# Sums over neighbours as seven half-size products in growing banks, in a two-layer graph kernel

## The chip, the cores and the metric

The kernel runs on one core of a Trainium2 chip. The metric is the device time of one execution in microseconds (us). Engines are named as in the profile: PE (TensorE), PEld (its weight loads), DVE (VectorE), ACT (ScalarE), POOL (GpSimd), SP (the queue that issues most transfers).

## What is computed

64 graphs of 256 nodes with 512 features, all in float32. With `ln` the layer norm, layer 0 is an attention masked by the adjacency matrix, layer 1 a graph convolution:

```
h = relu(ln(x));  q, k, v = h Wq' + bq, h Wk' + bk, h Wv' + bv
w = adj * exp(q k');  x = x + (w / rowsum(w)) v
h = relu(ln(x));  A = adj + I;  d = rowsum(A) ** -0.5
x = x + (d A d) (h W + b)          # d A d: rows and columns scaled by d
```

## The kernel before

**Tiles.** A round handles a pair of graphs (32 pairs, `p`). A pair's x is one tile of 128 partitions x 4 x 512: index t = 2 * node block + graph. The adjacency of the pair, `a`, and its transpose, `aT` (node block of the neighbour, graph, 256 nodes), are tiles too.

**Seven products.** Most matrix products are done on 2 x 2 blocks with seven block products in place of eight (the Winograd form). Sums of blocks (`s1..s4`, `t1..t4`) are made ahead of it, and the block results are put together from three PSUM banks. A bank "grows": a first product is written into it, somebody reads it, and a later product is added to the same bank. `seven_products` (L341) fixes the order: bank 0: A11, then A12; bank 1: S2, S3, A22; bank 2: S1, S4. After each product a callback reads the bank on ACT or DVE, and what the callback is told to start (`then_first`, `then_u2`, ...) is work for another pair, put into the queue behind that reading with `tc.issue_after`. [...]these callbacks set the order of all side work.

**Stages of pair p, in the order of TensorE.**

- `attend(p)` (L490): scores of both graphs in seven products of 128 columns (`pm_s`, L504), exponentials on ACT, masks with `aT` on DVE (L528), then eight tiles of weighted values (`pm_o`, L562). Then POOL adds the identity to the diagonal blocks of `aT` (L814), issues the transfer that adds the value bias to the next x, and makes the scale and offset of the second norm (`scale_offset`, L243: statistics on DVE, a chain of small POOL steps `irs_b` to `nb_b`, ending in L259).
- `project(p+1)` (L761): the key side (`pm_g`, seven products of 256 columns), and then the values (`pm_v`, seven products, `values` L429). Beside it: ACT's second norm of pair p (`h_b`, L266); statistics and degrees of pair p+2 on DVE and POOL (`irs_a` to `nb_a`); key sums on POOL (L334 to L338); ACT's first norm of pair p+2 (`h_a`); its transposes of 32 x 32 blocks on DVE (`hq`, L291), which ACT moves into place (`hT`, L310); four steps of key terms on DVE (`hc`, L280); and last, on DVE, the graph bias times the weighted degree, added to x of pair p (`add_graph_bias`, L610).
- `second_layer(p)`, `convolve` (L614): four sums over neighbours, each in a bank of its own (`pm_l`, L625), 16 matmuls of 256 columns; their sums (`yS`) on ACT and DVE; then seven products with the graph weight (`pm_w`, L358). Behind the last sum, t4, stands `weighted_degrees` of pair p+1 on DVE (`ad`, L593). In the products: ACT's scaled copies and the second half of the moves for pair p+2, POOL's additions to x (L667), DVE's scaled additions (L660), DVE's transposes of the next adjacency (`aT`, L475), then POOL's feature sums for pair p+2 (L320 to L324).

The last pairs differ: convolve(30) and convolve(31) follow each other, with the second norm of pair 31 in the former and its graph bias in the latter. In the first round the sums of the graph weight (L154 to L157), the weighted degrees of pair 0 and the transposed adjacency of pair 1 stand behind the value products on DVE. A tile's name after `tag=` is its slot: tiles of one tag share it, and a pool's `bufs` says how many slots there are. All PSUM tiles take turns in 8 banks.

## Time and profile before

| | |
|---|---|
| median of 3 runs | 1845.81 us (1845.35 to 1845.84) |
| the profiled execution | time 1845.12 us, span 1843.3 us |
| granted TensorE clock | 0.999 |
| one round, from attention to attention | 56.4 us (903.94 to 960.31) |
| of it `attend`: scores | 903.94 to 910.21 |
| weighted values | 910.21 to 917.14 |
| key side and values | 917.14 to 941.32 |
| sums over neighbours | 941.32 to 948.22 |
| graph weight's products | 948.22 to 960.31 |

The profile is of one execution. A timeline row has the start in us from the span's start, the length in us, the engine, the line and operation, what is written and read, the shape and how many instructions are merged in it; in brackets the idle time ahead of it and what ended that. A float32 matmul shows as two records, each with a weight load. Matmul ends are modelled and overlap the next start, so times of TensorE are read from start to start.

### The profile page before, as it was taken

The page shows a single profiled execution, that of the slowest core. Times are in us where ns is not written, and L with a number is a line of the kernel's source. Part 1 is how long each engine was busy: PE and PEld are TensorE (multiplying, and loading weights), DVE is VectorE, ACT ScalarE, POOL GpSimd, SP SyncE. Part 2 cuts the span into 40 slices and gives each one's busy share as a digit, 9 for nine tenths or more (in the row PEclk, how much of TensorE's full clock was granted, in tenths as well). Part 3 has the DMA queues.
Part 4 walks back from the last instruction along what each step waited for, and adds up shares of the span by engine and source line. Part 5 has one row for each costly group of instructions (what it writes and reads, how often), then busy time and mean ns, then how long its engine had stood idle before and what let it go on. Part 6 is the DMA issues. An engine that isn't in the chain of part 4 may idle for free.

```text
span 1843.3 us, 25928 instructions
## 1 busy us (share of the span) xinstructions
PE 1831.0 (99%) x9346; PEld 1632.8 (89%) x9346; DVE 1297.7 (70%) x3102; ACT 801.7 (43%) x1476; POOL 690.0 (37%) x867
## 2 busy tenths in 40 slices
PE   9999999999999999999999999999999999999999
PEld 8888888888888888888888888888888888888887
DVE  6877676676766767766767667677667677676755
ACT  4444444345434444443454344444434543444422
POOL 2433334333344333343333443433433334434332
PEclk9999999999999999999999999999999999999999
DMA  8343234332233432343422344223443223342111
GB/s 229 52 98 83 53 67 96 92 97 64 52 86 92 97 82 50 69 98 92 96 61 57 86 92 98 80 50 72 98 92 97 58 59 86 92 98 79 36 36 46
DMA packets 224192, 148.29 MB, mean 80 GB/s; under 512 B 150208, under 2 KB 170688, under 8 KB 224064
## 3 DMA queue, kind: packets, MB, share of 16 engines
q1 hardware_dynamic: 206048, 112.03, 22.2%
q0 software_dynamic: 16960, 33.56, 11.9%
q8 instruction: 74, 1.21, 0.3%
q10 hardware_dynamic: 1056, 1.05, 0.2%
q14 instruction: 54, 0.44, 0.1%
HBM read 112.99 MB, written 33.62 MB: 80 GB/s over the span
## 4 chain that ended last, share of the span: by engine, by line
PE 97%; DVE 1%; DMA 1%; issue 0%; POOL 0%; ACTq 0%; DVEq 0%
PE pm_w L358 21%; PE pm_g L358 21%; PE pm_v L358 20%; PE pm_o L562 12%; PE pm_l L625 12%; PE pm_s L504 11%; PE pm_mT L175 1%; DMA wq_rows<-in_L_gnn_Wq_w_dram 1%; DMA dflat<-irr_d 0%; DVE hc L280 0%; DVE ad L593 0%; DVE hq L291 0%; PE pt_h L300 0%; PE pt_wv L225 0%; DVE deg L578 0%
## 5 line engine op out<-in xcount | busy, mean ns | idle before, releaser
L358 PE MATMUL pm_w<-w_set,yS 128*128 128x256 f32 x1792 | 392.0, 379 | 0.0
L358 PEld LDWEIGHTS pm_w<-w_set,yS 128*128 128x128 f32 x1792 | 340.5, 190 | 46.3
L310 ACT COPY hT<-hq 32x512 f32<-32x512 f32 x496 | 305.4, 616 | 31.8 <-DVE hq L291 26.0
L358 PE MATMUL pm_v<-v_set,hT 128*128 128x256 f32 x1024 | 241.7, 379 | 0.0
L358 PE MATMUL pm_g<-hT,m_set 128*128 128x256 f32 x1024 | 236.7, 379 | 0.0
L667 POOL TENSOR_TENSOR x<-x,A_w 128x512 f32<-128x512 f32 x32 | 40.6, 1269 | 516.8 <-ACT A_w L658 516.8
L562 PE MATMUL pm_o<-v,wT 128*128 128x257 f32 (+1 forms) x1024 | 228.0, 380 | 0.0
L625 PE MATMUL pm_l<-aT,h_b 128*128 128x256 f32 x1024 | 226.2, 379 | 0.0
L358 PEld LDWEIGHTS pm_g<-hT,m_set 128*128 128x128 f32 x1024 | 194.5, 190 | 27.0 <-issue 0.5
L625 PEld LDWEIGHTS pm_l<-aT,h_b 128*128 128x128 f32 x1024 | 194.6, 190 | 26.5
L358 PEld LDWEIGHTS pm_v<-v_set,hT 128*128 128x128 f32 x1024 | 194.5, 190 | 26.4
L562 PEld LDWEIGHTS pm_o<-v,wT 128*128 128x128 f32 x1024 | 191.9, 190 | 26.8 <-DVE wT L528 0.3
L358 PE MATMUL pm_g<-hS,m_set 128*128 128x256 f32 x768 | 181.3, 379 | 0.0
L358 PE MATMUL pm_v<-v_set,hS 128*128 128x256 f32 x768 | 176.6, 379 | 0.0
L660 DVE SCALAR_TENSOR_TENSOR x<-pm_w,irr_d,x 128x256 f32<-128x256 f32 x256 | 110.9, 474 | 75.3 <-PE pm_w L358 75.3
L358 PEld LDWEIGHTS pm_g<-hS,m_set 128*128 128x128 f32 x768 | 145.4, 190 | 20.5 <-DVE U_g L398 0.3
L358 PEld LDWEIGHTS pm_v<-v_set,hS 128*128 128x128 f32 x768 | 145.8, 190 | 19.9
L390 ACT COPY A_g<-pm_g 128x512 f32<-128x512 f32 x32 | 18.7, 585 | 234.1 <-PE pm_g L358 233.4
L667 POOL TENSOR_TENSOR x<-x,U_w 128x512 f32<-128x512 f32 x64 | 81.2, 1269 | 102.0 <-DVE x L660 102.0
L266 ACT ACTIVATE h_b<-x,nb_b,rs_b 128x512 f32<-128x512 f32 x128 | 93.7, 803 | 47.6 <-POOL nb_b L259 47.6
L572 DVE SCALAR_TENSOR_TENSOR x<-pm_o,rsum,x 128x256 f32<-128x256 f32 x256 | 110.5, 473 | 2.0 <-DVE rsum L570 1.1
L436 ACT COPY A_v<-pm_v 128x512 f32<-128x512 f32 x32 | 18.7, 585 | 206.1 <-PE pm_v L358 197.1
(141 smaller groups left out, 2633.8 us busy)
## 6 DMA issues: line engine op xcount, KB each, us to landing
x<-in_x_dram SPq DMA_DIRECT2D x64, 512.0 KB, 4.9
x<-in_L_gnn_Wv_b_dram POOLq DMA_DIRECT2D x32, 1024.0 KB, 9.8
out_dram<-x SPq DMA_DIRECT2D x62, 512.0 KB, 3.0
a<-in_adj_dram SPq DMA_DIRECT2D x64, 256.0 KB, 2.9
aq<-in_adj_dram SPq DMA_DIRECT2D x124, 128.0 KB, 4.5
drow<-dflat SPq DMA_DIRECT2D x32, 256.0 KB, 4.7
wq_rows<-in_L_gnn_Wq_w_dram ACTq DMA_DIRECT2D x2, 512.0 KB, 7.5
wk_rows<-in_L_gnn_Wk_w_dram SPq DMA_DIRECT2D x2, 512.0 KB, 6.8
```

What stands on the lines that cost most here:

```text
L175: nc.tensor.matmul(pm, wk_rows[:, oc, ts(dc, P)], wq_rows[:, oc, ts(half, HD)], start=oc == 0, stop=oc == DC - 1,)
L266: nc.scalar.activation(h[:, t, :], x_tiles[p][:, t, :], AF.Relu, bias=nb[:, t : t + 1], scale=rd[:, t : t + 1],)
L310: last = nc.scalar.copy(dst[j * Q : (j + 1) * Q, i], src[i * Q : (i + 1) * Q, j])
L358: nc.tensor.matmul(banks[bank][:, r, :], left[:, ts(r, P)], right, start=start and r == 0 and dt == 0, stop=r == 1 and dt == 1, skip_group ...
L390: with tc.issue_after(nc.scalar.copy(a1, pm).ins):
L436: with tc.issue_after(nc.scalar.copy(a1, pm).ins):
L504: nc.tensor.matmul(banks[bank][:, g, :], left[:, dt, ts(g, P)], right[:, dt, ts(g, P)], start=start and g == 0 and dt == 0, stop=g == 1 an ...
L562: nc.tensor.matmul(pm[:, 0:width], wT[:, kb, qb, g, :], v[:, kb * G + g, lo : lo + width], start=kb == 0, stop=kb == NB - 1,)
L572: nc.vector.scalar_tensor_tensor(xh, pm[:, 0:HD], rsum, xh, mult, add)
L625: nc.tensor.matmul(pm[:, fi, :], h[:, jb * G + g, ts(2 * fh + fi, P)], aT[:, jb, g, :], start=jb == 0, stop=jb == NB - 1,)
L660: last = nc.vector.scalar_tensor_tensor(dst[:, r, :], pm[:, r, :], dr_, plus[:, r, :], mult, add)
L667: last = nc.gpsimd.tensor_tensor(block(i, g), block(i, g), more, add).ins
```

## The change

The sums over neighbours become seven products of half size, with new block sums on POOL (`neighbour_sums`), and are read from growing banks, in one hand-written order with the graph weight's products. In `convolve`, blocks of x are now taken by node block in place of by graph. `t3` and `t4` move from DVE to POOL. The weighted degrees of a pair move to its own value stage (`then_c22`), the graph bias to behind the key side. In the first round, the weighted degrees of pair 0 go into project(1), the transposed adjacency of pair 1 too, and the sums of the graph weight go to POOL. The scratch tiles of `hc` and `ad` take slot A0, the attention's small tiles become one tile in slot `hq`. The core of the diff:

```diff
-        scratch = p1.tile([P, D], F32, tag="scratch", name=f"hc_{p}")
+        scratch = p1.tile([P, D], F32, tag="A0", name=f"hc_{p}")
...
+        hold = p1.tile([P, 4, G, P], F32, tag="hq", name=f"hold_{p}")
-        first, u2, u3, c22 = (small(tag) for tag in ("sA", "sU2", "sU3", "sC"))
+        first, u2, u3, c22 = (hold[:, i] for i in range(4))
...
+    def neighbour_sums(p, h, aT):
+        a11, a21 = h[:, 0:G, 0:HD], h[:, 0:G, HD:D]
+        a12, a22 = h[:, G:TB, 0:HD], h[:, G:TB, HD:D]
+        gS = p1.tile([P, 3, G, HD], F32, tag="hbS", name=f"hbS_{p}")
+        s1, s2, s4 = (gS[:, i] for i in range(3))
+        b11, b12 = (aT[:, 0, :, ts(i, P)] for i in range(2))
+        b21, b22 = (aT[:, 1, :, ts(i, P)] for i in range(2))
+        aS = p1.tile([P, 3, G, P], F32, tag="aS", name=f"aS_{p}")
+        t1, t2, t4 = (aS[:, i] for i in range(3))
+        eng = nc.gpsimd
+        eng.tensor_tensor(t1, b12, b11, sub)
+        eng.tensor_tensor(t2, b22, t1, sub)
+        eng.tensor_tensor(s1, a21, a22, add)
+        eng.tensor_tensor(s2, s1, a11, sub)
+        eng.tensor_tensor(a21, a11, a21, sub)
+        eng.tensor_tensor(b12, b22, b12, sub)
+        eng.tensor_tensor(t4, b21, t2, sub)
+        eng.tensor_tensor(s4, a12, s2, sub)
+        return (a11, a12, a22, s1, s2, a21, s4), (b11, b21, b22, t1, t2, b12, t4)
...
-        pm11 = aggregate(0, 0)
-        with tc.issue_after(moved) if moved else ExitStack():
-            nc.scalar.copy(b11, pm11)
-        pm12 = aggregate(0, 1)
-        nc.vector.tensor_tensor(t1, pm12, b11, sub)
-        pm22 = aggregate(1, 1)
-        nc.scalar.copy(b22, pm22)
-        nc.vector.tensor_tensor(t2, pm22, t1, sub)
-        nc.vector.tensor_tensor(t3, b22, pm12, sub)
-        pm21 = aggregate(1, 0)
-        nc.scalar.copy(b21, pm21)
-        with tc.issue_after(nc.vector.tensor_tensor(t4, pm21, t2, sub).ins):
-            then_t4()
...
+        def gather(bank, left, right, start=False):
+            if start:
+                banks[bank] = ps_m.tile([P, 2, G, P], F32, tag="pm", name=f"pm_l_{p}_{bank}")
             for fi in range(2):
+                for g in range(G):
                     nc.tensor.matmul(
+                        banks[bank][:, fi, g, :],
+                        left[:, g, ts(fi, P)],
+                        right[:, g, :],
...
+        chain = gather(0, a11, c11, True)
+        with tc.issue_after(moved) if moved else ExitStack():
+            nc.scalar.copy(b11, chain)
+        pm = gather(1, a12, c21, True)
+        nc.vector.tensor_tensor(b11, pm, b11, add)
+        gather(0, s2, u2)
+        nc.vector.tensor_tensor(part, chain, b11, sub)
+        rest = gather(2, s1, u1, True)
+        gather(0, s3, u3)
+        nc.scalar.copy(three, chain)
+        pm0 = product(0, A11, b11, True)
+        nc.vector.tensor_tensor(b22, rest, three, add)
+        nc.scalar.copy(a, pm0)
+        gather(0, a22, u4)
+        nc.scalar.copy(b21, chain)
+        gather(2, s4, c22)
+        nc.vector.tensor_tensor(t1, rest, part, add)
+        last = nc.vector.tensor_tensor(t2, b22, t1, sub)
+        nc.gpsimd.tensor_tensor(t3, t2, b11, sub)
+        turned = nc.gpsimd.tensor_tensor(t4, b21, t2, sub)
+        with tc.issue_after(last.ins):
+            then_t2()
+        scaled(a1, a, 1)
+        last = scaled(a, a, 0)
+        with tc.issue_after(turned.ins):
             into(1, 0, None, a)
+        with tc.issue_after(last):
+            then_first()
+        product(0, A12, b21, False)
+        into(0, 0, pm0)
+        pm2 = product(2, S1, t1, True)
+        pm1 = product(1, S2, t2, True)
+        s2, s3 = (temp(tag, f"w{p}") for tag in ("U2", "U3"))
+        scaled(s2, pm1, 1, a1)
+        into(0, 1, None, s2)
+        product(1, S3, t3, False)
+        with tc.issue_after(scaled(s3, pm1, 1, a1)):
+            then_u3()
+        into(1, 1, pm2)
+        last = into(1, 1, None, s3)
+        product(1, A22, t4, False)
+        into(1, 0, pm1)
+        product(2, S4, b22, False)
+        into(0, 1, pm2)
...
     def project(p, then_g):
+        def then_u2():
+            ahead(measure, p + 1)()
+            if p == 1:
+                weigh_degrees(0)
+        keys[p], last = key_side(p, parts[p], then_g, then_u2, nothing)
+        with tc.issue_after(last):
+            add_graph_bias(p - 1)
         key_parts[p] = key_sums(p, keys[p])
+        if p == 1:
+            weight_sums(w1_set, w1_21, nc.gpsimd)
+        def then_c22():
+            if p == 1:
+                aTs[1] = transposed_adjacency(1)
+            weigh_degrees(p)
-        last = values(
+        values(
...
             then_u3=ahead(find_terms, p + 1),
+            then_c22=then_c22,
         )
-        with tc.issue_after(last.ins):
-            add_graph_bias(p - 1)
...
     def finish_second_norm(p):
-        second[p] = normed(p, f"b{p}", *norms[p])
+        second[p] = neighbour_sums(p, normed(p, f"b{p}", *norms[p]), aTs[p])
```

The scheduler that places the instructions keeps this order on DVE, ACT and POOL with small shifts: on DVE the four `hc`, the four `ad` and three value steps stand between U_v (s3) and `b11`'s addition, and on POOL the order after `nb_b` is s1, s2, the difference in a21, s4, then `irs_a` to `nb_a`, then the key sums.

## Prediction

> **What bounds the kernel now.** I read the page's busy shares and chain first, then the TensorE timeline of one middle pair, then VectorE's and GpSimd's timelines of that pair, and last the one place where TensorE really waits, the first pair.

> ```profile
> PE 1831.0 (99%) x9346; PEld 1632.8 (89%) x9346; DVE 1297.7 (70%) x3102; ACT 801.7 (43%) x1476; POOL 690.0 (37%) x867
> ...
> PE 97%; DVE 1%; DMA 1%; issue 0%; POOL 0%; ACTq 0%; DVEq 0%
> PE pm_w L358 21%; PE pm_g L358 21%; PE pm_v L358 20%; PE pm_o L562 12%; PE pm_l L625 12%; PE pm_s L504 11%; PE pm_mT L175 1%; DMA wq_rows<-in_L_gnn_Wq_w_dram 1%; DMA dflat<-irr_d 0%; DVE hc L280 0%; DVE ad L593 0%; DVE hq L291 0%; PE pt_h L300 0%; PE pt_wv L225 0%; DVE deg L578 0%
> ```

> TensorE sets the end, and it is full: only fewer streamed columns can help, and any new wait costs in full. The TensorE timeline of a middle pair (start, length, then line and tiles) prices the columns:

> ```profile
> 903.94 1.05 PE L504 MATMUL pm_s<-hT,gT 128*128 128x128 f32 x8
> 904.83 1.95 PE L504 MATMUL pm_s<-hS,gS 128*128 128x128 f32 x16
> ...
> 941.32 7.07 PE L625 MATMUL pm_l<-aT,h_b 128*128 128x256 f32 x32
> 948.22 12.25 PE L358 MATMUL pm_w<-w_set,yS 128*128 128x256 f32 x56
> ```

> From start to start, 8 records of 128 columns take 0.89 us (112 ns each; a float32 matmul is two records), 32 of 256 columns take 6.90 (216 ns each). So half-width costs a little over half.

> **The gain.** The sums over neighbours were 32 records of 216 ns = 6.90 us a pair. They become seven products of 4 matmuls of 128 columns: 56 x 112 = 6.27 us. Gain 0.63 us a pair, 32 x 0.63 = 20 us. The other products are the same in number and width. Without new waits this would give 1825 us.

> **The waits that pay for it.** Before, every neighbour sum had its own bank and TensorE asked nobody. Now bank 0 grows: it is read by ScalarE (b11), by VectorE (`part`), by ScalarE (`three`), each time before TensorE may go on. So VectorE's queue ahead of `part` comes onto TensorE's path. In it stand the four key terms hc (L280), and now also the weighted degrees (ad, L593), moved there from behind t4. VectorE and GpSimd in this stretch before:

> ```profile
> 936.34 0.69 DVE L448 TENSOR_TENSOR U_v<-pm_v,A_v 128x512 f32<-128x512 f32 x1 [0.31 <-PE pm_v L358]
> 936.95 0.68 DVE L280 SCALAR_TENSOR_TENSOR hc<-h_a,c_all 128x512 f32<-128x512 f32 x1
> ...
> 925.43 0.23 POOL L238 TENSOR_SCALAR irs_a<-mv_a 128x4 f32<-128x4 f32 x1 [4.28 <-DVE mv_a L250]
> ...
> 928.12 0.20 POOL L259 TENSOR_TENSOR nb_a<-nm_a,irr_a 128x4 f32<-128x4 f32 x1
> 930.88 1.27 POOL L334 TENSOR_TENSOR gS<-gT 128x512 f32<-128x512 f32 x1 [2.57 <-DVE gT L409]
> ...
> 934.71 1.26 POOL L338 TENSOR_TENSOR gS<-gT,gS 128x512 f32<-128x512 f32 x1
> ```

> The key sums on GpSimd (L334 to L338) end at 935.97, one microsecond before the first hc. That gap matters, as the first pair shows, where feature sums on GpSimd run beside hc and ad:

> ```profile
> 53.99 1.66 DVE L280 SCALAR_TENSOR_TENSOR hc<-h_a,c_all 128x512 f32<-128x512 f32 x1
> ...
> 56.21 1.12 DVE L280 SCALAR_TENSOR_TENSOR hc<-h_a,c_all 128x512 f32<-128x512 f32 x1
> ...
> 53.83 1.27 POOL L320 TENSOR_TENSOR hS<-hT 128x512 f32<-128x512 f32 x1 [11.42 <-ACT hT L310]
> 55.18 1.60 POOL L321 TENSOR_TENSOR hS<-hT,hS 128x512 f32<-128x512 f32 x1
> ...
> 59.21 1.16 PE L504 MATMUL pm_s<-hT,gT 128*128 128x128 f32 x8 [2.54 <-DVE sU L533]
> ```

> An hc of 0.68 us takes 1.66: it starts 0.16 after L320 and ends 0.55 after it. The next is held to the end of L321. [...]for operands from PSUM and for the block transposes, which overlap GpSimd's sums in every pair, it shows no lengthening. [...]

> Now the middle pair's timetable, in the times of before. GpSimd's queue: after nb_b come four neighbour sums, which wait for ScalarE's h_b (ends 924.12). Priced as the key sums (5.09), they end at 929.3. Only then follow irs_a to nb_a (2.89 before, from 925.43). VectorE's bias step (4 STT, 2.73 us as L610) now runs at 930.7 to 933.4, directly after the key side. It holds back irr_d and nb_a (0.7 together, the nearest being the small GpSimd steps of the first pair, lengthened by 0.2 to 0.5 each): nb_a ends near 933.0 instead of 928.3. Hence
> - the key sums run from 933.3 to about 938.35, over the first hc;
> - ScalarE's h_a (began 931.68) begins at 933.05, so the four transposes end at 936.8 instead of 936.0, and U_v (s3) starts at 936.7 instead of 936.34;
> - the first hc would start at 937.3, is held to 938.2 and ends 938.9; the second 939.6; c22 (0.69) ends at 940.25. TensorE's last value product reuses c22's bank and would start at 939.59. Wait 0.7, with restart **0.8 us**. (A restart after a short wait costs 0.07: at 1793.1, after 0.62 us idle, one matmul took 185 ns and the next 112.)
> - then hc 0.73, hc 0.61, c21 0.61, ks 0.22, ad 0.46 and 0.36, c12 0.61, ad 0.46 and 0.47, s 0.19, b11 0.61, ds 0.19, `part` 0.69: `part` ends at 946.4. TensorE, restarted at 940.4, has the product (1.73) and four gathers (3.58) and is there at 945.7. Wait 0.7, with restart **0.8 us**. Were no GpSimd step in the way, the same sum from 936.34 would end at 945.1 against 944.9: 0.3 us remain.
> - b21: the last gather of bank 0 is copied by ScalarE (0.585), which has just done a's copy and one scaling (0.58 + 0.43); it ends about 0.1 after TensorE's next gather. **0.2 us** (0 to 0.3).
> - the A22 product waits for VectorE's reading of s3 (two STT, 0.88) behind half a product: **0.1 us** (0 to 0.2).
> - In the attention, the first adjacency sum (128x256: 0.73 us, estimated between 0.46 for 128x128 and 1.27 for 128x512) enters GpSimd right after the first two diagonals, at 910.70; the mask of block (1,0) came at 910.80. If the sum is first, the mask ends 0.45 later, and pm_o's fourth matmul waits 0.35; if the mask is first, the sum holds the next masks and the statistics behind them, and all of the chain above comes later. **0.3 us** (0 to 0.45).

> Sum 2.2 us of waits against 0.63: +1.57 a pair, for the 29 pairs with this order (it is the same in all of them): +45.5 us.

> Costed at nothing: t3 and t4 moved to GpSimd (2 x 1.27, idle there, a product of 1.73 ahead of S3; without that cover 1.2 us), the fifth VectorE step, scratch tiles sharing A0 and hq (same engines), the output and load DMAs (same order on SP; x is not read sooner). h_b is not held up: the other adjacency sums end near 916.5, and irs_b comes at 919.06.

> The ends. The first pair loses work from VectorE: its attention waits 2.54 and 1.64 us, and then runs at half rate (213 ns per record) for about 2 us, 6.4 us in all. But the graph weight's sums go to GpSimd, 4 x 1.27 beside the same hc, so I take 3 of it (0 to 6.4). Pair 0's own sums follow a longer VectorE queue (two more transposes, 1.3): +2. Pair 30 has no hc ahead of it: -0.3. In pair 31 the bias (2.73) stands between t2 and the steps that free bank 1, and t3, t4 on GpSimd interleave with it: about 3.3 of wait, net +2.7 (0 to 3.5). Together +1.4.

> The sum is made against the profiled execution: span 1843.3, time 1845.1, which is 0.7 below the median of the runs, 1845.8. 1845.1 + 45.5 + 1.4 = **1892 us**.

> **Rivals.**
> - *A, as above*, 1870 to 1915: chance 0.62.
> - *B, the queues miss each other*: the key sums end before hc, and the masks go first. Left are 0.3 (`part`), 0.2, 0.1, 0.3 = 0.9, net +0.3 a pair: 29 x 0.3 + 1.4 = +10, 1855 (1847 to 1870). For it: the gap between sums and hc is one microsecond now. Against: GpSimd's order puts 5.1 us ahead of nb_a. Chance 0.20.
> - *C, faster: the gain comes through*. If VectorE reaches `part` by 944.9, no bank is late, and 20 us are gained, with the first pair's 3 to 6: 1820 to 1825, up to 1841 with a part of it. It decides at one place, the start of the third gather into bank 0: VectorE must be 0.3 us earlier than the best that I find. For it: all other growing banks (pm_g, pm_v, pm_w, pm_s) run without waits. Against: none of them has hc and ad ahead of it. Chance 0.09.
> - *D, worse*: a key sum gets in ahead of the fourth bias step; U_v (s2) is then 1.2 later, at 935.2, and the value product on bank 1 (934.41) waits 0.85 more: 29 x 0.85 = +25, 1917 (1915 to 1935). Chance 0.09.

> That the change does not do what it says is excluded by the matmuls of its program: 28 of 128 columns a pair.

> **Numbers.** The range 1850 to 1920 takes A whole, most of B and a little of D; about 2 in 10 stay out. A measurement tells about 0.2% (3.7 us) from no change. Faster 0.09 (C), within 0.2% 0.04 (B's lower end), slower 0.87.

> **What would show it.** TensorE busy near 1811 with 60 or more us of idle; rows of waits "pm_v <- v" at the last value product and "pm_l <- U_l" at the third gather of bank 0, each about 0.7 us in some 29 places; hc's mean up from 697 to about 900 ns; pm_l records 112 ns apart. Wrong: no idle before pm_l, or hc at 0.68 throughout (B or C); idle ahead of pm_v's S3 product (D).

## The result and the profile after

The changed kernel takes **1896.78 us** (median of four runs, 1895.71 to 1898.62), beside 1845.82 of the kernel before on the same chip (1845.35 to 1847.0): a ratio of 1.0276 (95% interval 1.0258 to 1.0294), slower. The profiled execution has a span of 1894.9 us against 1843.3, 51.6 more, at a granted clock of 0.997. The forecast was 1892.

The busy shares and the chain of the page of after:

```profile
PE 1852.5 (98%) x10114; PEld 1642.0 (87%) x10114; DVE 1358.7 (72%) x3130; ACT 797.9 (42%) x1476; POOL 1070.3 (56%) x1191
...
PE 73%; DVE 25%; issue 1%; POOL 1%; DMA 1%; ACT 0%; DVEq 0%; ACTq 0%; POOLq 0%
```

TensorE had 97% of the chain and now has 73%; the 25% that VectorE took over are its queue, followed back from where TensorE waits for it in every pair (a share of the chain, not the length of the waits). Now TensorE's timeline of the same middle pair (its key side begins 21.38 us later than before):

```profile
961.38 1.99 PE L358 MATMUL pm_v<-v_set,hT 128*128 128x256 f32 x8 [0.25 <-DVE v L458]
963.21 1.95 PE L654 MATMUL pm_l<-aT,h_b 128*128 128x128 f32 x16
965.03 2.02 PE L654 MATMUL pm_l<-aS,hbS 128*128 128x128 f32 x16
967.37 1.13 PE L654 MATMUL pm_l<-aT,h_b 128*128 128x128 f32 x8 [0.31 <-DVE U_l L696]
```

16 records of 128 columns take 1.82 us from start to start, so the half-size products do run at their price. Two brackets are new, and they stand where the forecast put them: ahead of the last value product and ahead of the third gather of bank 0. The brackets undercount: the modelled end of a record of 256 columns lies 0.16 us behind the start of the next, and the second record after a wait comes late too (by 0.10 and 0.07 here). From start to start the two waits are 0.53 and 0.55 us. VectorE and GpSimd in this pair:

```profile
958.37 0.67 DVE L281 SCALAR_TENSOR_TENSOR hc<-h_a,c_all 128x512 f32<-128x512 f32 x1
...
959.09 1.63 DVE L281 SCALAR_TENSOR_TENSOR hc<-h_a,c_all 128x512 f32<-128x512 f32 x1
...
960.65 0.68 DVE L458 TENSOR_TENSOR v<-pm_v,U_v 128x512 f32<-128x512 f32 x1
...
966.53 0.69 DVE L696 TENSOR_TENSOR U_l<-pm_l,yS 128x512 f32<-128x512 f32 x1
...
953.62 0.54 POOL L260 TENSOR_TENSOR nb_a<-nm_a,irr_a 128x4 f32<-128x4 f32 x1
954.12 1.78 POOL L335 TENSOR_TENSOR gS<-gT 128x512 f32<-128x512 f32 x1
...
958.46 1.71 POOL L339 TENSOR_TENSOR gS<-gT,gS 128x512 f32<-128x512 f32 x1
```

The last key sum (L339, 1.71 us where it took 1.26 before) is held by the first hc and then holds the second: it ends at 960.17, and that hc, begun at 959.09, takes until 960.72. c22 (L458) starts when hc is done, and the value product behind it; `part` (U_l) ends at 967.22, and the third gather starts 0.15 later. Over the whole run (us in total, times, longest):

```profile
PE pm_l L654 <- DVE U_l L696: 10.6, 30, 1.2
PE pm_v L358 <- DVE v L458: 7.5, 29, 0.3
```

One round by stages, each the mean over 26 middle pairs from the start of a record to the start of the next (so a wait is counted in the stage of the record before it; worked out from the trace; "v3" comes further below):

```
us per pair             pm_o   pm_g   pm_v   pm_l   pm_w   pm_s   period
before                  6.93  12.09  12.09   6.91  12.09   6.27   56.37
after                   7.32  12.09  12.61   6.99  12.34   6.37   57.72
e1 key sums later       7.32  12.09  12.10   6.65  12.34   6.37   56.87
e2 mask first           6.93  12.09  12.61   6.99  12.34   6.37   57.33
e3 split product        7.32  12.09  12.61   6.43  12.34   6.37   57.16
e4 no block sums        6.93  12.09  16.04   6.61  12.34   6.37   60.38
e5 ends                 7.32  12.09  12.61   6.97  12.34   6.37   57.71
e6 c22 first            7.32  12.09  12.09   6.42  12.35   6.37   56.63
e10 same, order kept    7.32  12.09  12.09   6.78  12.34   6.37   56.98
e7 degrees back         7.32  12.10  12.64   6.64  16.32   6.41   61.42
e8 same, other slot     7.32  12.09  12.61   6.64  14.14   6.37   59.17
e9 norm first           6.93  12.09  16.49   7.20  12.34   6.37   61.42
v3 all                  6.93  12.09  12.09   6.43  12.14   6.26   55.95
```

After minus before is +1.345 a pair, 39 us over 29 pairs. The other 12.6 lie at the ends: 2.3 up to the second pair's weighted values (the first pair's start 2.7 earlier, then 5.0 are lost), 1.8 between pairs 30 and 31, 7.6 from there to the last product, 0.9 behind it. Each of e1 to e10 below is one run; the kernel before gave 1845.1 to 1846.3 beside them.

### The profile page after: what moved, and what is told of

Same layout as the page of the kernel before. It is cut to its first block, busy times and chain, and to the rows that moved or that the text cites. A ratio compares the mean times of both kernels' runs of the same rounds, so it can differ in the third digit from the quotient of the medians.

```text
span 1894.9 us, 27986 instructions
## 1 busy us (share of the span) xinstructions
PE 1852.5 (98%) x10114; PEld 1642.0 (87%) x10114; DVE 1358.7 (72%) x3130; ACT 797.9 (42%) x1476; POOL 1070.3 (56%) x1191
## 3 DMA queue, kind: packets, MB, share of 16 engines
q10 hardware_dynamic: 1056, 1.05, 0.2%
## 4 chain that ended last, share of the span: by engine, by line
PE 73%; DVE 25%; issue 1%; POOL 1%; DMA 1%; ACT 0%; DVEq 0%; ACTq 0%; POOLq 0%
PE pm_w L358 21%; PE pm_g L358 20%; PE pm_s L511 10%; PE pm_o L566 10%; DVE hc L281 6%; PE pm_v L358 6%; PE pm_l L654 5%; DVE hq L292 4%; DVE ad L597 3%; DVE x L614 2%; DVE wT L532 1%; DVE U_l L696 1%; DVE yS L694 1%; DVE U_v L446 1%; DVE v L472 1%; DVE v L471 1%
## 5 line engine op out<-in xcount | busy, mean ns | idle before, releaser
L358 PE MATMUL pm_w<-w_set,yS 128*128 128x256 f32 x1792 | 413.2, 386 | 3.8 <-DVE U_w L674 3.8
L358 PEld LDWEIGHTS pm_w<-w_set,yS 128*128 128x128 f32 x1792 | 332.4, 191 | 57.3 <-issue 10.4
L708 POOL TENSOR_TENSOR yS<-yS 128x512 f32<-128x512 f32 x32 | 41.1, 1284 | 410.1 <-DVE yS L707 410.1
L358 PE MATMUL pm_v<-v_set,hT 128*128 128x256 f32 x1024 | 245.2, 382 | 10.3 <-DVE v L458 7.5
L358 PE MATMUL pm_g<-hT,m_set 128*128 128x256 f32 x1024 | 238.5, 381 | 4.2 <-DVE gT L415 4.2
L566 PE MATMUL pm_o<-v,wT 128*128 128x257 f32 (+1 forms) x1024 | 235.3, 382 | 3.5
L358 PEld LDWEIGHTS pm_v<-v_set,hT 128*128 128x128 f32 x1024 | 192.3, 190 | 47.5 <-DVE v L458 19.2
L358 PEld LDWEIGHTS pm_g<-hT,m_set 128*128 128x128 f32 x1024 | 195.7, 191 | 31.9 <-DVE gT L415 5.0
L358 PE MATMUL pm_g<-hS,m_set 128*128 128x256 f32 x768 | 181.2, 379 | 1.0 <-DVE U_g L404 1.0
L358 PE MATMUL pm_v<-v_set,hS 128*128 128x256 f32 x768 | 176.8, 379 | 0.0
L358 PEld LDWEIGHTS pm_g<-hS,m_set 128*128 128x128 f32 x768 | 145.7, 190 | 21.3 <-DVE U_g L404 1.4
L358 PEld LDWEIGHTS pm_v<-v_set,hS 128*128 128x128 f32 x768 | 146.0, 190 | 19.7
L684 POOL TENSOR_TENSOR x<-x,U_w 128x512 f32<-128x512 f32 x64 | 81.0, 1267 | 93.5 <-DVE U_w L674 93.5
L674 DVE SCALAR_TENSOR_TENSOR U_w<-pm_w,irr_d,A_w 128x256 f32<-128x256 f32 x128 | 56.0, 480 | 98.8 <-PE pm_w L358 98.8
L281 DVE SCALAR_TENSOR_TENSOR hc<-h_a,c_all 128x512 f32<-128x512 f32 x128 | 115.9, 905 | 2.0
L654 PE MATMUL pm_l<-aT,h_b 128*128 128x128 f32 x768 | 98.6, 278 | 10.6 <-DVE U_l L696 10.6
```

Of the source, the lines that this page charges most:

```text
L281: nc.vector.scalar_tensor_tensor(scratch, h[:, t, :], 1.0, c_all, mult, mult, accum_out=acc[:, t : t + 1])
L358: nc.tensor.matmul(banks[bank][:, r, :], left[:, ts(r, P)], right, start=start and r == 0 and dt == 0, stop=r == 1 and dt == 1, skip_group ...
L566: nc.tensor.matmul(pm[:, 0:width], wT[:, kb, qb, g, :], v[:, kb * G + g, lo : lo + width], start=kb == 0, stop=kb == NB - 1,)
L654: nc.tensor.matmul(banks[bank][:, fi, g, :], left[:, g, ts(fi, P)], right[:, g, :], start=start and fi == 0 and g == 0, stop=fi == 1 and g ...
L674: last = nc.vector.scalar_tensor_tensor(dst[:, r, :], pm[:, r, :], dr_, plus[:, r, :], mult, add)
L684: last = nc.gpsimd.tensor_tensor(block(i, nb), block(i, nb), more, add).ins
```

## The experiments

**Theory T.** The half-size products themselves are cheaper (16 records in 1.82 us). What costs is a meeting on two engines: the neighbour sums push the key sums on GpSimd later (1.9 us at their start, 2.8 at their end), over hc on VectorE, and there VectorE's steps with two SBUF inputs and GpSimd's sums hold each other up, as seen above: hc takes 1.63 us in place of 0.68, the key sum 1.71 in place of 1.26. VectorE's steps that read PSUM and its block transposes were not held in the kernel before: U_v (L440) took 0.69 us in all 32 pairs, in 31 of them beside a GpSimd sum, and the 124 transposes (L291) 0.67 to 0.71, 120 of them beside such sums. VectorE then comes late to two readings that TensorE now waits for. **Rival R:** VectorE has simply got too much work ahead of `part`, or GpSimd has too many sums, wherever they lie.

### e1: the key sums elsewhere

```diff
-        nc.vector.tensor_tensor(ds, s, d, mult)
+        last_ds[0] = nc.gpsimd.tensor_tensor(ds, s, d, mult).ins
...
-        key_parts[p] = key_sums(p, keys[p])
...
+        with tc.issue_after(last_ds[0]):
+            key_parts[p] = key_sums(p, keys[p])
```

The new place is behind `values(p)`; the other small step of the degrees, `s`, goes to GpSimd in the same way.

> The changed kernel with the four key sums on GpSimd issued later, behind the last step of the weighted degrees (some 945 to 949 in the pair's timetable, where GpSimd is idle), in place of beside bias, hc and U_v; the last two small steps of the degrees (128x4) go to GpSimd to give that place in the queue. Everything else is as changed. Theory T (the key sums exclude hc on VectorE; that is what makes TensorE wait at the last value product and at the third gather of bank 0): hc back to 0.70 us mean from 0.905, the wait ahead of the last value product (0.52 a pair) and that ahead of pm_l (0.55 a pair) both go, 1.07 x 29 = 31 us less than the changed kernel's 1897: 1866. Rival R (VectorE simply has too much to do ahead of `part`; who runs beside it does not matter): only the two small steps are saved, 1893.

Measured: 1867.22 us. hc in the groups by line (busy us, mean ns, idle before), and the first key sum in GpSimd's timeline:

```profile
L282 DVE SCALAR_TENSOR_TENSOR hc<-h_a,c_all 128x512 f32<-128x512 f32 x128 | 89.4, 699 | 2.0
```

```profile
949.86 1.27 POOL L336 TENSOR_TENSOR gS<-gT 128x512 f32<-128x512 f32 x1
```

hc is at 699 ns again (905 in the changed kernel), and the key sums take 1.26 or 1.27 each. In the changed kernel the last, held by hc, took 1.71, and the first 1.78, beside the last step of the bias. pm_v's wait is gone whole, pm_l's but for 0.22. With all of the change's work still in place this is 29.5 of 51 us: T, not R. T's 31 us were right in sum, not in parts: the middle pairs give 24.7, since those 0.22 stay, and the stretch up to the second pair's weighted values 3.4. The forecast had 0.3 remain "were no GpSimd step in the way". What keeps them is not the queue, though: VectorE idles 0.42 ahead of its sum of b11 (949.76), for TensorE's own second gather, and `part` comes behind that sum.

### e2: the masks ahead of the first adjacency sum

```diff
-        eng.tensor_tensor(t1, b12, b11, sub)
+        with tc.issue_after(diagonals[p]):
+            eng.tensor_tensor(t1, b12, b11, sub)
```

> The changed kernel with the first adjacency sum on GpSimd issued behind the last of the diagonal additions, so that the masks' inputs are never behind it. Theory T (the sum stands between a diagonal and its mask; pm_o waits 0.38 us in 31 pairs): the waits of pm_o on wT go, 0.38 x 31 = 12 us less: 1885. Rival: the sum comes later and so do irs_b, the second norm and the chain behind it, what pm_o gains comes back at pm_v or pm_l: 1897 again.

Measured: 1885.15 us, pm_o at 6.93, every other stage as in the changed kernel. The last three masks on VectorE and the sum on GpSimd, first after, then e2:

```profile
931.79 1.62 DVE L532 TENSOR_TENSOR wT<-wT,aT 128x256 f32<-128x256 f32 x3
...
931.73 0.72 POOL L629 TENSOR_TENSOR aS<-aT 128x256 f32<-128x256 f32 x1
```

```profile
924.54 1.22 DVE L532 TENSOR_TENSOR wT<-wT,aT 128x256 f32<-128x256 f32 x3
```

A mask has two SBUF inputs. The sum starts 0.06 ahead of the first of the three, and they take 0.40 longer: they are held as hc was, at a second place. Its 11.6 us did not come back anywhere.

### e3: half a product as cover

```diff
+        product(0, A11, b11, True, (0,))
         gather(0, s3, u3)
         nc.scalar.copy(three, chain)
-        pm0 = product(0, A11, b11, True)
+        pm0 = product(0, A11, b11, False, (1,))
```

> The changed kernel with the A11 product of the graph weight (4 matmuls, 1.73 us) split: its first half is put ahead of the third gather of bank 0, which waits for `part`, the other half stays where it was. So `part` gets 0.86 us more cover, and the later reading of bank 0 (`three`, ahead of the fourth gather) loses as much. Theory T (the wait at the third gather is 0.55 a pair, and three's copy has spare cover): wait gone but for 0.05 to 0.1, some 0.47 x 29 = 14 us less: 1883. Rival (the wait only moves to the fourth gather, since its cover is halved): 1897.

Measured: 1878.16 us, 5 better than T said. pm_l falls to 6.43, and the wait ahead of the third gather is gone altogether. The fourth gather now has a short one, for ScalarE's copy `three`; it shows in the weight loads:

```profile
PEld pm_l L654 <- ACT U_l L700: 6.8, 32, 0.3
```

The loads are 0.2 us late, the records 0.07: half a product is all but enough for `three`. 6.43 is 0.47 less than the four sums before, where 0.63 had been worked out. The missing 0.16 are not spread over the products. In a middle pair, records come late at three places only: two behind ScalarE's copy of b11 (0.04 and 0.07 over 112 ns, both also in the changed kernel) and one behind `three` (0.07). Products that start without such a reading ahead of them show nothing. So the price of the columns was right.

### e4: without the added sums

```diff
-        eng.tensor_tensor(t1, b12, b11, sub)
-        eng.tensor_tensor(t2, b22, t1, sub)
-        eng.tensor_tensor(s1, a21, a22, add)
...
+        s1, s2, s4, t1, t2, t4 = a22, a12, a12, b21, b22, b21
```

> Leaves out the eight block sums on GpSimd of the new neighbour stage (the products take other blocks in their place, so the neighbour sums are not those of the reference); TensorE's work, VectorE's and ScalarE's are as in the changed kernel. It takes 5 + 3 us of GpSimd's work away from the stretch ahead of the key side's end. Theory T (what counts is which VectorE steps the GpSimd sums meet, not how many there are): without them the key sums begin as soon as gT is there, at about 930.9 in the pair's timetable and so together with bias (930.7), alternate with its four steps, the reading U_v (s2) comes to some 936.8 and the value product on bank 1 (934.4) waits 2 to 3 us, while hc is free (0.70): 1930 to 1945. Rival (the added GpSimd work is the cost): the waits go, 1850 to 1857.

Measured: 1967.06 us. **Less work on GpSimd, and 70 us slower than the changed kernel.** VectorE, GpSimd and TensorE in a middle pair:

```profile
985.17 5.78 DVE L614 SCALAR_TENSOR_TENSOR x<-b_all,ds,x 128x512 f32<-128x512 f32 x4
...
985.40 1.65 POOL L335 TENSOR_TENSOR gS<-gT 128x512 f32<-128x512 f32 x1 [2.57 <-DVE gT L415]
...
991.61 1.99 PE L358 MATMUL pm_v<-v_set,hT 128*128 128x256 f32 x8 [2.52 <-DVE U_v L446]
```

The key sums start with the bias and the two queues take turns: the four key sums take 1.60 to 1.71 us each instead of 1.27, the bias's four steps 5.78 us instead of 2.73, U_v comes 3 us late, the value product on bank 1 waits 2.52. That is rival D of the forecast in full. The size was missed: behind such a wait TensorE runs a few records at half rate (last section), which makes pm_v 3.95 longer instead of 2 to 3. hc is free (0.69), as T said.

### e5: the ends

```diff
-        last = nc.vector.tensor_tensor(t2, b22, t1, sub)
...
-        with tc.issue_after(last.ins):
-            then_t2()
...
+        with tc.issue_after(nc.vector.tensor_tensor(part, chain, b11, sub).ins):
+            then_part()
...
+        def then_first():
+            then_g()
+            if p == 1:
+                weigh_degrees(0)
```

The callback is the bias of the last pair in the first part; the second part stands in `project`.

> The changed kernel with only its ends altered: in the last pair the graph bias (four VectorE steps with two SBUF inputs) is put behind `part` instead of behind t2, where t3, t4 and additions to x run on GpSimd; the weighted degrees of pair 0 are put ahead of the key side's statistics in project(1), so that they don't meet the neighbour sums of pair 0. The regular pairs are unchanged (period 57.72). Theory T (bias and GpSimd's steps let each other in one by one, and TensorE runs its next records at half rate after such a long wait): 44.8 us to the last product in place of 52.4 or near it (some -6.7), the first pair some -5: 1885. Rival (the ends cost what they do because the pairs overlap less there): 1897, or -2 at most.

Measured: 1890.54 us, half of it. The last stretch is 5.6 us shorter, 46.9. The last pair of the changed kernel, in which the bias stood beside t3, t4 and an addition to x:

```profile
1874.20 5.77 DVE L614 SCALAR_TENSOR_TENSOR x<-b_all,ds,x 128x512 f32<-128x512 f32 x4
...
1874.43 1.65 POOL L708 TENSOR_TENSOR yS<-yS 128x512 f32<-128x512 f32 x1 [8.25 <-DVE yS L707]
...
1882.08 4.18 PE L358 MATMUL pm_w<-w_set,yS 128*128 128x256 f32 x9 [3.84 <-DVE U_w L674]
```

Again turns, 5.77 for 2.73, then a wait of 3.84 and nine records in 4.18 us, about half rate. The first pair gave nothing: pair 1 is 3.2 shorter (58.9), but the first weighted values start 3.4 later (64.6). The degrees came forward into the first attention, where feature sums run on GpSimd: two ad take 0.96 and 1.37, and even the two steps of 128x4 take 1.03 and 1.18 (0.15 otherwise), so a reading of scores is late and TensorE waits 2.67.

### e6 and e10: c22 ahead of hc

```diff
+            ahead(find_terms, p + 1)()
...
-            then_u3=ahead(find_terms, p + 1),
+            then_u3=nothing,
```

The first line stands in `then_c22`; `find_terms` is the four hc.

> The changed kernel with c22 (the reading that frees the bank of the last value product) ahead of the four key terms hc on VectorE instead of behind the second. Nothing else changes. Theory T (both waits have one cause, VectorE's queue from U_v to `part`, which is late by the time that the key sums held hc): the wait at the last value product goes (pm_v 12.61 back to 12.09), but TensorE now comes 0.5 us earlier to the third gather and waits for the same `part`, so pm_l takes 0.5 to 0.9 more: 1897 to 1909. Rival (the two waits are separate): only pm_v's goes, 1882.

Measured: 1866.11 us. Neither: both waits go. VectorE in a middle pair:

```profile
944.42 0.69 DVE L458 TENSOR_TENSOR v<-pm_v,U_v 128x512 f32<-128x512 f32 x1 [0.99 <-PE pm_v L358]
945.03 0.68 DVE L281 SCALAR_TENSOR_TENSOR hc<-h_a,c_all 128x512 f32<-128x512 f32 x1
```

VectorE now idles 0.99 us for the product that c22 reads, and the first hc comes at 945.03, behind the last key sum (ends 944.70 here). So it gives away as much as the hold had taken (0.94), and TensorE still waits for nothing. Two other things had moved with it in the orders planned from the program. One ad and the degrees' two small steps fell behind `part`, so U_v to `part` is 8.03 instead of 8.74 us. And on TensorE one matmul of the A11 product (0.43 us) came ahead of the third gather, a quarter of e3's edit. e10 takes the latter back:

```diff
-        pm0 = product(0, A11, b11, True)
+        with tc.issue_after(gathered[0].ins):
+            pm0 = product(0, A11, b11, True)
```

`gathered[0]` is the last matmul of the third gather.

> As the run with c22 ahead of the key terms, but with TensorE's order kept as in the changed kernel: in that run one of the four A11 matmuls of the graph weight (0.43 us) had come ahead of the third gather in the order that was planned from the program, which the edit had not meant. Worked out from that run's trace: `part` starts at 950.80 and ends at 951.49; TensorE ended its second half gather at about 951.35 and would now go on to the third gather at once. If the A11 matmul was what hid the rest of the wait: 0.2 to 0.35 us of wait at the third gather come back, pm_l 6.65 to 6.8 in place of 6.42, pm_v stays 12.09: 1866 + 29 x 0.3 = 1873 to 1878. If the matmul did not matter: 1866. If the whole wait moves there (my expectation of that run): 1897.

Measured: 1873.01 us, pm_l 6.78, pm_v 12.09. So the wait at the value product is c22's place behind hc, as forecast; of the wait at the third gather 0.36 us come back without the matmul that e6 had let ahead. My expectation of e6, that the whole wait moves on to `part`, is refuted. The rest of that wait was paid by the shorter queue, which e10 has too (8.03 us); no run has the order of c22 alone, without it.

### e7 and e8: the degrees back behind t2

```diff
         def then_c22():
             if p == 1:
                 aTs[1] = transposed_adjacency(1)
-            weigh_degrees(p)
+                weigh_degrees(1)
...
+            if p > 0:
+                then_t2 = lambda: weigh_degrees(p + 1)
```

> The changed kernel with the weighted degrees (four ad and two small steps, 1.8 us of VectorE) moved back behind t2, as before the change; the graph bias stays behind the key side. Theory T: `part` no longer waits behind ad, so the wait at the third gather goes (-0.55 x 29 = -16 us), the one at the last value product stays; but behind t2 the four ad now meet t3 and t4, which the change put on GpSimd, and each is held up to the end of a GpSimd step: some 3 to 4 us later on VectorE for the readings of the graph weight's products, a wait of 1 us or more there. In all 1895 to 1930. Rival (place does not matter, only the amount ahead of `part`): 1881.

Measured: 2009.71 us. The third gather's wait falls (pm_l 6.64), by 0.35 of the 0.55 expected, and pm_w pays 3.98. But not for my reason:

```profile
1028.04 0.43 DVE L597 SCALAR_TENSOR_TENSOR ad<-a,drow 128x256 f32<-128x256 f32 x1 [2.41 <-POOL x L684]
...
1026.73 1.27 POOL L684 TENSOR_TENSOR x<-x,A_w 128x512 f32<-128x512 f32 x1
```

No ad is held: they take 0.42 each. The first one doesn't start, since its scratch tile shares slot A0 with A_w, which the third GpSimd step (L684) reads until 1028.0. The slot, which the forecast had costed at nothing where ad stands now, costs 2.4 us here. e8 gives ad another slot:

```diff
-        scratch = p1.tile([P, N], F32, tag="A0", name=f"ad_{p}")
+        scratch = p1.tile([P, N], F32, tag="U3", name=f"ad_{p}")
```

> As the run before with the weighted degrees moved back behind t2, but their scratch tile takes slot U3 (written and read by VectorE alone) in place of A0. In that run the first ad did not start for 2.41 us, until GpSimd had done t3, t4 and the addition that reads the tile in A0, and then each ad took 0.42: that looks like a wait for the slot and not like the exclusion that I had expected. If it is the slot: ad now starts right behind t2 at once and runs beside t3 and t4; by the exclusion the two then alternate (ad 1.0 to 1.4 each, as in the first pairs of the changed kernel, end some 1 us earlier than there), pm_w waits some 1 us less and is seldom at half rate: period 58 to 59.5, 1905 to 1950. If ad and GpSimd don't exclude each other: all ad done by 1.9 us after t2, pm_w as in the changed kernel, pm_l 6.64: 1881 to 1886. If the slot has nothing to do with it: 2010 again.

Measured: 1942.09 us, period 59.17, as the slot's theory said. Now ad and GpSimd's steps hold each other up instead (ad 1.08 and 1.37 us for 0.42 in e7, L684 1.45 for 1.27):

```profile
996.28 1.08 DVE L597 SCALAR_TENSOR_TENSOR ad<-a,drow 128x256 f32<-128x256 f32 x1
997.40 1.37 DVE L597 SCALAR_TENSOR_TENSOR ad<-a,drow 128x256 f32<-128x256 f32 x1
...
997.04 1.45 POOL L684 TENSOR_TENSOR x<-x,A_w 128x512 f32<-128x512 f32 x1
```

So with t3 and t4 on GpSimd the degrees are worse off where they were: behind t2 they cost 1.8 us in pm_w, and save 0.35 at the third gather.

### e9: the statistics ahead of the neighbour sums

```diff
+            with tc.issue_after(last_nb[0]), tc.issue_after(last_root[0]):
+                second[p - 1] = neighbour_sums(p - 1, second[p - 1], aTs[p - 1])
```

> The changed kernel with the chain irs_a to nb_a (statistics of the next pair) ahead of the new neighbour sums on GpSimd; all eight block sums come behind it, and so behind the key side's statistics. Tests the step that 5.1 us of sums ahead of nb_a on GpSimd make ScalarE's h_a and with it the transposes late. Theory T: h_a is early again, but the sums run beside bias, hc and ad instead, so VectorE is held more: 1925 to 1960, hc's mean above 1.0 us. Rival (the late chain is what costs): less than the changed kernel's 1897.

Measured: 2001.56 us. nb_a is early, but all sums then run beside bias (mean 1370 ns, 800 in the changed kernel) and hc (1106), the value product on bank 1 waits 2.2 us a pair and the last one 0.9 to 1.35. The direction is T's. Of the 42 us above 1960 some 13 are half rate again (last section); the rest is waiting that the forecast put too low. The late chain cost less than the sums do here.

### v3: all mendings

e1, e2, e3 and e5 together, and in the graph weight's products (core):

```diff
+        with tc.issue_after(behind):
+            scaled(a1, a, 1)
+            last = scaled(a, a, 0)
...
         product(0, A12, b21, False)
-        pm2 = product(2, S1, t1, True)
         pm1 = product(1, S2, t2, True)
+        pm2 = product(2, S1, t1, True)
         product(1, S3, t3, False)
-        product(1, A22, t4, False)
         product(2, S4, b22, False)
+        product(1, A22, t4, False)
```

`behind` is the copy of b21.

> All mendings together: key sums later, masks first, the A11 product split, the ends altered, and two more: b21's copy ahead of the scalings on ScalarE, and the graph weight's products in the order A12, S2, S1, S3, S4, A22, so that each reading of a growing bank has a whole product beside it. Expected from the stages: pm_o 6.93, pm_g, pm_v, pm_w 12.09 each, pm_l 6.43, pm_s 6.27, a period of 55.90 against 56.37 of the kernel before: 29 x 0.47 = 13.7 us less, with the ends (first pair -2, last +1 to +3) 1831 to 1834. Rival (each mended wait comes back one place later): 1841 to 1850, no better than before.

Measured: **1830.36 us** (median of five, 1830.12 to 1830.97) beside 1846.34 of the kernel before (nine runs): ratio 0.9915, 95% interval 0.9902 to 0.9929, and just below the 1831 to 1834 expected. The page's busy shares and chain of v3:

```profile
PE 1816.4 (99%) x10114; PEld 1635.4 (89%) x10114; DVE 1305.0 (71%) x3066; ACT 801.7 (44%) x1476; POOL 1053.4 (58%) x1255
...
PE 97%; DVE 1%; ACT 1%; POOL 0%; issue 0%; DVEq 0%; ACTq 0%; POOLq 0%
```

VectorE's busy time falls from 1358.7 to 1305.0 us, though only two small steps a pair have left it: the rest of the 53.7 was mostly holding (those steps took 0.15 to 0.17 us each, some 10 in all; hc falls from 115.9 to 88.5 us, the bias from 94.5 to 87.3). The chain is TensorE's again, and the period 55.95, with 55.90 expected.

## Why the prediction was right, and where its terms were off

Sum: 1892 for 1896.78, from case A. The mechanism of case A is what happened, but that the sum came within 5 us is in part luck: the middle pairs were put 6.5 us too high and the ends 11.2 too low. What held: the place of both waits and their cause, GpSimd's order, the timetable (with the 21.38 us of shift, nb_a was to end at 954.4 and did at 954.2; h_a was to start at 954.4 and did at 954.2; the key sums were to end at 959.7 and did at 960.2), hc's mean (about 900 ns; 905), records 112 ns apart. One sign did not come: TensorE's busy time was to be near 1811 with 60 us or more of idle, and is 1852.5 with 42, as the profile counts part of each wait (0.24 us of the 0.55 at the third gather), and the records at half rate (427 ns apart in place of 216), as busy. The forecast carried the holding of hc and ad in the first pair of before (1.66 us for 0.68, 1.14 for 0.42) over to the middle pairs; that the bias and the masks would be held too was my estimate then, and the runs showed it (bias 5.78 us for 2.73 in e4, three masks 1.62 in the changed kernel and 1.22 in e2).

```
us a pair                       forecast   measured   by
gain of the half-size products   -0.63      -0.47     e3 (0.16 of short waits in it)
wait at the last value product    0.8        0.53     after, e1, e10
wait at the third gather          0.8        0.55     after, e3
b21 and A22                       0.3        0.36     pm_w + pm_s, after; 0.05 left in v3
masks                             0.3        0.38     e2
net                               1.57       1.345
x 29                             45.5       39.0
ends                              1.4       12.6      e5 for the last pair alone
```

- **The gain** was priced rightly by its columns. Of the readings of bank 0 that the forecast lists, it gave a wait to `part` alone and one to b21; the copies of b11 and, in e3 and v3, of `three` cost the missing 0.16.
- **The two large waits** were over-sized by a third each. I had the first hc held to 938.2 and all else moved with it; in fact the first got in, held the last key sum, and the second was held. Their common origin was right (e1 removes the first whole and the second but for 0.22), and that c22 stands behind hc too (e10).
- **Rival C** put the point at which the gain comes through at 0.3 us of VectorE ahead of `part`. e3 and v3 confirm that it is this place: with 0.86 us of cover the third gather waits for nothing.
- **The ends** were the term that failed. For the last pair I took t3, t4 and bias to "interleave with it: about 3.3 of wait, net +2.7". They do take turns, and the wait is 3.84; but with the slower records behind it, the wait at `part` (1.3) and what lies around, it comes to 7.6. For pair 0's sums I took +2 for a longer queue and overlooked that the degrees and the bias of pair 0 run beside pair 0's neighbour sums: three ad at 1.01 to 1.37, a bias of 3.75 us, and a wait of 2.81 on the key side with half rate behind it; 5.0 in all. This is read from the trace and not shown by e5, whose own waits took up what it gained there. And pair 30 to 31, costed at -0.3, has a new wait of 2.2 for U_v.
- **Costed at nothing**, rightly in the middle pairs: t3 and t4 on GpSimd. The slot A0 was costed at nothing too, and is so only as long as ad isn't near `a` (e7).

## What to carry to other kernels

When work is moved to GpSimd, list which VectorE steps with two SBUF inputs it will meet, step by step in time, not how busy the engines are: here hc took 905 ns in the mean where the key sums met it and 699 where they did not (after, e1), less GpSimd work in a worse place cost 70 us (e4), and the same work in a better place gave 30 (e1). When a product is made to grow in a bank, give every reading of the bank other work of TensorE beside it: 0.86 us more of it took away the wait of 0.55 for `part`, and half a product left the records behind `three` 0.07 us late (e3). A reordering of five products, together with an earlier copy of b21 on ScalarE, gave another 0.3 us a pair (v3; the two were not run apart). Before an edit is costed at nothing, look whom its tile shares a slot with (2.4 us in e7), and compare the planned orders for what else has moved (0.36 us a pair between e6 and e10).

## What the runs showed of the hardware

```profile
932.17:935.58 3.41, 3.41 (x10) 0.50 0.24 77
991.60:995.01 3.41, 3.40 (x16) 1.00 0.37 71
```

Counted over each run, waits from start to start (the ends of the run left out):

```
wait, us            where               waits   followed by clock 0.50   records
0.9 to 1.35         e9, last value        29      0
1.76                e8, pm_w              29      0
2.2                 e7, nearly all pm_w   30     28                      6 to 8
2.19                e9, pm_v              30     17                      6 to 8
2.68                e4, pm_v              29     20                      7 to 8
```

Six to eight records at +211 ns are 1.3 to 1.7 us, so a wait of 2.2 us cost up to 3.9, and one of 1.76 (e8) only itself. Within one run, pairs with such a stretch can be set beside pairs without: in e4 they take 60.88 us instead of 59.26, in e7 61.43 instead of 59.77 (one pair only), in e9 61.78 instead of 61.00, since the waits that follow there get shorter. In all that is 32 us of e4, 47 of e7 and 13 of e9: the whole of e4's excess over its expectation, over half of e7's (80) and a third of e9's (42). It shows in the mean granted clocks (0.981, 0.972, 0.984; e8 0.998).

What sets equal waits apart can be read from the starts of these stretches. In these three runs they lie whole multiples of 3.413 us apart, to within 1 ns. In the changed kernel those at 81.559, 1880.383 and 1894.036 us lie 527 and 4 steps of 3.4133 us apart, in the kernel before those at 62.028 and 1843.785 lie 522 apart. The three runs and e8 have 120 waits longer than 1.5 us, taken from the modelled end of a record to the next start. Of them 65 have 1.96 us or more inside one step of 3.413 us, counted from these starts, and all were followed by the half clock; 55 have less, and none was. In the changed kernel the wait of 2.81 us has 2.61 inside one step; that of 2.08 for U_v (1821.84 to 1823.91) has 1.55, and the clock behind it is 1.00. In the kernel before, the wait of 2.54 us (56.67 to 59.21) has 1.94 in its first step, and the next step (58.61 to 62.03) ran at 1.00. What makes the steps was not shown.

**Turns.** In e4 two full queues, one of VectorE steps with two SBUF inputs and one of GpSimd sums, let each other in one by one: 2.73 us of bias became 5.78, and GpSimd's 1.27 became 1.60 to 1.71. VectorE's own two-input steps of 128x4 were held too (1.03 and 1.18 us in place of 0.15, e5).
